# Four experts in two stages: gated products of one expert ahead of the return of the one before, and the rotation's scaling pinned later

## The chip, the cores and the metric

The kernel runs on one core of one Trainium2 chip. Its metric is the time of one execution on the device, in microseconds (us). A core has five engines that run their own queues in order: TensorE (PE, matrix products; PEld is its loading of weights), VectorE (DVE), ScalarE (ACT), GpSimd (POOL) and SyncE (SP, which issues most of the DMAs here). They wait for each other through semaphores. Products are written to PSUM, everything else lies in SBUF or in HBM.

## The reference

Two transformer-like layers on x of 4 x 512 x 512. The first adds a test-time-training attention and a ternary FFN; the second adds a latent attention (MLA) with 16 heads and a rotation of half of each head, and a feed-forward with four experts, where row n goes to expert n mod 4. What the change touches is that last part:

```python
def _L1_ffn_ref(x, gate_up_proj, down_proj):
    B, N, H = x.shape
    E, _, two_I = gate_up_proj.shape
    I = two_I // 2
    x4 = x.reshape(B, N // E, E, H)
    gu = jnp.einsum('bgeh,ehd->bged', x4, gate_up_proj)
    gate, up = (gu[..., :I], gu[..., I:])
    inter = jax.nn.silu(gate) * up
    out = jnp.einsum('bgei,eih->bgeh', inter, down_proj)
    return out.reshape(B, N, H)
...
x = x + _L1_attn_ref(xn, ...) + _L1_ffn_ref(xn, ...)
```

Here E = 4, H = I = 512, all in float32. In the attention, queries and keys are rotated with cos and sin tables before the scores, and the scores are scaled by 1/sqrt(128).

## The kernel before, in words

`trunk_kernel` has three parts: the first layer (to L774), the expert stage (L870 to L983) and the heads of the attention (from L989). The expert stage computes the second layer's feed-forward into four tiles `y[b]`, and beside it prepares what the heads need.

For expert e, `product` (L904) multiplies 128 columns of the weight tile `gu` (512 x 1024, gate and up halves) with the expert's rows `xe`: four matmuls of 512 columns into one PSUM tile, eight rows in the profile. For each of four blocks i there is a gate product `epg` and an up product `epu`; ACT takes the SiLU of the first into `esg` (L950), and VectorE multiplies with the second into `inter` (L951). Then the return: for each batch b, four matmuls of `inter` with the second weight `dn` into `epo` (L957), and VectorE adds that to `y[b]` (L964). So the order on TensorE is products 0, return 0, products 1, return 1, and so on.

Buffers: `epg`, `epu`, `esg`, `inter`, `epo` and `dn` have two each, `gu` of even and of odd experts one each. A product into a buffer waits until the one two places before it has been read: `epu` of block i + 2 waits for `inter` of block i.

The order of most instructions on an engine is chosen by a scheduler when the kernel is built; matmuls of the heads are pinned to the order of the text (`pin`), and so are the large loads of this stage (`fetch`, L880: `xe`, `gu`, `dn`, `y`). All DMAs from SP and ACT take turns on eight completion semaphores: a DMA is issued only when the one eight places ahead of it has landed.

Beside the experts, `if e == 1` (L924) loads what the heads need: `wqr`, `wkr`, biases, the cosine and sine table `trig_k` in four loads (L934), the latents `ckv` and `cq` from `lat_d`, which the first layer's end writes, and starts `first`, a generator (`fold`, L811) that folds the rotations into the heads' weights. `fold` loads straight parts `uk` and `uq` (L816), then five times 16 small loads `raw` (L845), which VectorE transposes into `wt` (L835; one buffer each), and small products `pw` and `pvo` on TensorE; `ow` (L822) are rows of the output weight. After return 1, L969 to L977 put the biases through the rotation and make `trig_q` as `trig_k` times `scale` (L977); it depends on nothing but `trig_k`. It is first read by the heads' `rotate` (L1003).

Of the kernel before, what the change touches and what calls it, by code (L numbers as in the profile page):

```python
# [12 lines left out]
F32 = mybir.dt.float32  # L13
AF = mybir.ActivationFunctionType
# [4 lines left out]
P = 128  # L19
B, L, HS = 4, 512, 512  # L20
# [24 lines left out]
H, D, KVC, QC, RD = 16, 128, 128, 384, 64  # L45
# [6 lines left out]
E, EI = 4, 512  # L52
# [3 lines left out]
def trunk_kernel(ctx: ExitStack, tc: tile.TileContext, a: dict, out: bass.AP):  # L56
    nc = tc.nc
# [20 lines left out]
    def rows_of(ap, b):  # L78
        return ap[b].rearrange("(j e) d -> j e d", e=E)
# [9 lines left out]
    with ExitStack() as px:  # L89
        one = px.enter_context(tc.tile_pool(name="b_one", bufs=1))  # L90
        wk = px.enter_context(tc.tile_pool(name="b_wk", bufs=2))
# [301 lines left out]
        def queries_out(n, wh):  # L393

            po = ps_st.tile([P, NC, 4, K + 1], F32, tag="pso", name=f"pso_{n}")
            for b, r in enumerate(quarters):
                for be in range(NC):
                    mm(po[r, be, :, :K], wh[:, 4 * b + be, :], wq_bd[:, 4 * b + be, :, HD:], be == 0, False)
            return po
# [352 lines left out]
        for n in range(NM):  # L752
            wh = weights_out(n)
            pz = first_product(n, pre)
            po = queries_out(n, wh)
# [25 lines left out]
    y = [ypool.tile([P, E, HS], F32, tag=f"y{b}", name=f"y{b}") for b in range(B)]  # L781
# [5 lines left out]
    scale = 1.0 / math.sqrt(D)  # L787
    trig_k = lat.tile([P, L], F32, tag="trig_k", name="trig_k")
    trig_q = lat.tile([P, L], F32, tag="trig_q", name="trig_q")
# [80 lines left out]
    with ExitStack() as px:  # L870
        one = px.enter_context(tc.tile_pool(name="d_one", bufs=1, reuse_waits="tile"))
        wd = px.enter_context(tc.tile_pool(name="d_wd", bufs=2, reuse_waits="tile"))
        wg = px.enter_context(tc.tile_pool(name="d_wg", bufs=1, reuse_waits="tile"))
        wk = px.enter_context(tc.tile_pool(name="d_wk", bufs=2, reuse_waits="tile"))
        psp = px.enter_context(tc.tile_pool(name="d_ps", bufs=2, space=PSUM))
        ps_gu = px.enter_context(tc.tile_pool(name="d_psgu", bufs=2, space=PSUM))
        gate_w = [one.tile([P, NC, 2 * EI], F32, tag="gu1", name="gu_1")]
        gate_w.insert(0, wg.tile([P, NC, 2 * EI], F32, tag="gu0", name="gu_0"))

        def fetch(**kw):  # L880

            tc.keep_in_program_order(nc.sync.dma_start(**kw))

        def gates(e):
            gu = gate_w[e] if e < 2 else (wg, one)[e % 2].tile([P, NC, 2 * EI], F32, tag=f"gu{e % 2}", name=f"gu_{e}")
            fetch(out=gu, in_=a["gu"][e].rearrange("(c p) o -> p c o", p=P))
            return gu

        def downs(e):
            dn = wd.tile([P, EI // P, HS], F32, tag="dn", name=f"dn_{e}")  # L890
            fetch(out=dn, in_=a["dn"][e].rearrange("(c p) o -> p c o", p=P))
            return dn

        gu = gate_w[0]
        nc.gpsimd.dma_start(out=gu, in_=a["gu"][0].rearrange("(c p) o -> p c o", p=P))
        xe = wg.tile([P, 2 * NCHUNK, NC, E, 32], F32, tag="xe", name="xe")
        for k in range(2 * NCHUNK):
            if k < 2 * NCHUNK - 2:
                nc.gpsimd.dma_start(out=xe[:, k], in_=xe_d[k])
            else:  # L900
                fetch(out=xe[:, k], in_=xe_d[k])
        ws = {0: (gu, downs(0))}

        def product(e, ps, w, col):  # L904
            for c in range(NC):
                nc.tensor.matmul(  # L906
                    ps, lhsT=w[:, c, col : col + P], rhs=xe[:, :, c, e, :], start=(c == 0), stop=(c == NC - 1)
                )

        def by_chunk(ap):  # L910

            return ap.rearrange("p (k b j) -> p k b j", k=NCHUNK, b=B)

        def by_batch(ap):

            return ap.rearrange("p b (k j) -> p k b j", k=NCHUNK)

        for b in range(B):
            fetch(out=y[b], in_=rows_of(yd, b))
        for e in range(E):  # L920
            gu, dn = ws.pop(e)
            if e + 1 < E:
                ws[e + 1] = gates(e + 1), downs(e + 1)
            if e == 1:  # L924
                nc.sync.dma_start(out=wqr, in_=a["W_QR"])
                nc.sync.dma_start(out=wkr, in_=a["W_KR"])
                buv16 = wk.tile([H, D], F32, tag="buv16", name="buv16", bufs=1)
                nc.sync.dma_start(out=buv16, in_=a["b_UV"].rearrange("(h d) -> h d", d=D))
                w0 = group_tiles(lat, 0)
                first = fold(w0, 0, wk, lambda nm: psp.tile([P, 512], F32, tag="pa", name=nm), 1)  # L930
                nc.sync.dma_start(out=buk, in_=a["b_UK"])
                nc.sync.dma_start(out=buq, in_=a["b_UQ"])
                for k in range(E):
                    nc.sync.dma_start(  # L934
                        out=trig_k[RD:, :].rearrange("p (k e j) -> p k e j", k=NCHUNK, e=E)[:, :, k],
                        in_=a["trig"][:, k * P : (k + 1) * P].rearrange("p (k j) -> p k j", k=NCHUNK),
                    )
                nc.sync.dma_start(out=ckv, in_=lat_d[0].rearrange("p b k x -> p b (k x)"))
                for i in range(QC // P):
                    nc.sync.dma_start(out=cq[:, i], in_=lat_d[1 + i].rearrange("p b k x -> p b (k x)"))  # L940
            inter = wk.tile([P, EI // P, B * P], F32, tag="inter", name=f"inter_{e}")
            for i in range(EI // P):
                if e > 1:
                    next(first, None)
                pg = ps_gu.tile([P, B * P], F32, tag="pg", name=f"epg_{e}_{i}")
                product(e, pg, gu, i * P)
                pu = ps_gu.tile([P, B * P], F32, tag="pu", name=f"epu_{e}_{i}")
                product(e, pu, gu, EI + i * P)
                sg = wk.tile([P, B * P], F32, tag="sg", name=f"esg_{e}_{i}")
                nc.scalar.activation(sg, pg, AF.Silu)  # L950
                nc.vector.tensor_mul(  # L951
                    by_batch(inter[:, i].rearrange("p (b j) -> p b j", b=B)), by_chunk(pu), by_chunk(sg)
                )
            for b in range(B):
                po = psp.tile([P, HS], F32, tag="po", name=f"epo_{e}_{b}")
                for i in range(EI // P):
                    nc.tensor.matmul(  # L957
                        po,
                        lhsT=inter[:, i, b * P : (b + 1) * P],
                        rhs=dn[:, i, :],  # L960
                        start=(i == 0),
                        stop=(i == EI // P - 1),
                    )
                nc.vector.tensor_add(y[b][:, e, :], po, y[b][:, e, :])  # L964
            if e in (1, 2):
                next(first, None)
            if e == 1:

                for wr, bias in ((wkr, buk), (wqr, buq)):  # L969
                    pb = psp.tile([P, 512], F32, tag="pa", name="pb")  # L970
                    nc.tensor.matmul(pb[RD:, :H], lhsT=wr, rhs=bias, start=True, stop=True)
                    nc.vector.tensor_copy(bias[RD:, :], pb[RD:, :H])
                pb = psp.tile([P, 512], F32, tag="pa", name="pbuv")
                nc.tensor.transpose(pb[:, :H], buv16, ident[:H, :H])
                nc.vector.tensor_copy(buv, pb[:, :H])
                nc.vector.tensor_scalar_mul(buq[:RD, :], buq[:RD, :], scale)
                nc.vector.tensor_scalar_mul(trig_q[RD:, :], trig_k[RD:, :], scale)  # L977
            if e == 2:
                for b in range(B):
                    pt = psp.tile([P, E, P], F32, tag="pa", name=f"lv_tr_{b}")  # L980
                    for k in range(E):
                        nc.tensor.transpose(pt[:, k, :], ckv[:, b, k * P : (k + 1) * P], ident)
                    nc.scalar.copy(lv[:, b], pt)  # L983

# [2 lines left out]
    with ExitStack() as px:  # L989
        wk = px.enter_context(tc.tile_pool(name="e_wk", bufs=2, reuse_waits="tile"))  # L990
# [145 lines left out]
        ws, cs, qk, probs = {}, {}, {}, {}  # L1136
        folds, outs = iter(()), []
        ws[0] = w0
        for i in range(nu + 1):
            if i < nu:  # L1140
                hg, b, h = units[i]
# [15 lines left out]
            if i >= 3:  # L1157
                hg, b, h = units[i - 3]
# [9 lines left out]
            if 0 <= k < HPG * B:  # L1168
                b, e = divmod(k, HPG)
                nc.gpsimd.tensor_add(y[b][:, e, :], y[b][:, e, :], bo)  # L1170

        b = B - 1
        at = ws[NHG - 1], cs[NHG - 1, b]
        po = {}
# [106 lines left out]
```

## Time and profile before

| | us |
|---|---|
| median of three runs | 2126.29 (2125.87 to 2128.31) |
| the profiled run's own time | 2126.91 |
| its span, first to last instruction | 2125.1 |
| expert stage on TensorE, first `epg` to first `pk` of the heads | 1008.48 to 1193.54 |
| VectorE / ACT / POOL busy, share of the span | 56% / 40% / 24% |
| DMA landing, median: `gu` 2 MB, `dn` 1 MB, `y` 1 MB | 7.8, 5.3, 10.3 |

The page gives one profiled execution. A row of a timeline has the start from the span's beginning, the length, the engine (a q behind it marks its queue, where DMAs are issued), the line, operation, output and inputs, the count, and in brackets the idle time before it with what ended it. A row of the waits has who waited for whom, the sum, how often, and the longest. A wait for several semaphores is put down to the one that came last.

### The profile page before, as it was taken

Reading aid. Unit: us, or ns where it says so; the run is one execution under the profiler, and the core shown is the slowest. Engines: PE = TensorE matmul, PEld = TensorE weight load, DVE = VectorE, ACT = ScalarE, POOL = GpSimd, SP = SyncE. Lnnn points to the kernel's source line nnn. Section 1 sums busy time; section 2 is a strip of 40 time slices with the busy share of each in tenths; the row PEclk is TensorE's granted clock in tenths of the full one; section 3 lists DMA queues with packets and bytes.
Section 4 is the critical chain, followed back from the end, with each engine's and each line's share of the span. In section 5 each row is a group of like instructions: output and inputs, shape, how many; then the busy total and the mean of one; then the engine's idle time right before and its main releaser. Section 6 shows DMA issues by size and latency. Waiting matters only on the chain.

```text
span 2125.1 us, 29355 instructions
## 1 busy us (share of the span) xinstructions
PE 2041.5 (96%) x9932; PEld 1169.6 (55%) x9932; DVE 1199.9 (56%) x2452; ACT 860.5 (40%) x1733; POOL 504.4 (24%) x555
## 2 busy tenths in 40 slices
PE   8999999999999998997899999999999999999999
PEld 6777777767676765744344344444444444444444
DVE  5445656565737475633111485766666665766663
ACT  2334343434334343312001364555545554555552
POOL 5233333323333332302000121111111111142110
PEclk9999999999999999999999999999999999999999
DMA  6546464645454646445831143443334333433332
GB/s 187 161 133 185 120 190 116 193 114 174 138 165 127 183 120 200 116 123 178 300 98 29 29 99 79 93 98 79 78 81 106 78 80 73 101 78 76 91 96 75
DMA packets 336496, 257.19 MB, mean 121 GB/s; under 512 B 107099, under 2 KB 264988, under 8 KB 335324
## 3 DMA queue, kind: packets, MB, share of 16 engines
q1 hardware_dynamic: 322320, 243.89, 42.8%
q10 hardware_dynamic: 11500, 5.32, 0.9%
q0 software_dynamic: 2528, 6.12, 0.8%
q8 instruction: 80, 1.31, 0.3%
q14 instruction: 68, 0.56, 0.1%
HBM read 159.50 MB, written 29.62 MB: 89 GB/s over the span
## 4 chain that ended last, share of the span: by engine, by line
PE 78%; DVE 6%; SPq 6%; DMA 4%; ACT 3%; issue 2%; POOL 1%; ACTq 0%; DVEq 0%; POOLq 0%
PE pj L100 14%; PE pf L100 11%; PE po L1119 9%; PE pc L1106 8%; PE sc L1038 8%; PE pq L1028 7%; PE pd L100 5%; SPq L1098 4%; PE epo L957 3%; PE epu L906 2%; PE pso L100 2%; PE pk L1020 2%; PE epg L906 2%; PE pz L100 2%; SPq L845 1%
## 5 line engine op out<-in xcount | busy, mean ns | idle before, releaser
L1013 POOL TENSOR_TENSOR kT<-t_k,t_k 32x512 f32<-32x512 f32 x64 | 80.7, 1260 | 802.6 <-PE pq L1028 339.9
L1043 ACT ACTIVATE prob<-sc,mx 128x512 f32<-128x512 f32 x256 | 174.3, 683 | 198.9 <-DVE mx L1040 194.1
L1038 PE MATMUL sc<-kT,qT 96*128 96x512 f32 x512 | 230.9, 593 | 1.7 <-ACT prob L1043 1.4
L1119 PE MATMUL po<-vo,ctxT 128*128 128x512 f32 x512 | 230.0, 592 | 0.7 <-ACT ctxT L1108 0.7
L1106 PE MATMUL pc<-prT,lv 128*128 128x512 f32 x496 | 224.8, 596 | 3.2 <-DVE t_q L1003 3.2
L1067 DVE STREAM_TRANSPOSE tt<-prob 128x512 f32<-128x512 f32 x252 | 173.0, 706 | 56.2 <-ACT prob L1048 48.5
L1028 PE MATMUL pq<-cq,uq 128*128 128x512 f32 x384 | 178.0, 600 | 7.3 <-ACT ctxT L1108 7.3
L100 PE MATMUL pf<-xT,wg 128*128 128x256 f32 x704 | 173.5, 389 | 8.2 <-DVE hid L459 7.1
L1048 ACT ACTIVATE prob<-prob,sm 128x512 f32<-128x512 f32 x256 | 176.4, 713 | 0.0
L1040 DVE TENSOR_REDUCE mx<-sc 128x1 f32<-128x512 f32 x256 | 168.2, 678 | 5.8 <-PE sc L1038 3.8
L100 PE MATMUL pf<-xT,wu 128*128 128x256 f32 x704 | 167.5, 381 | 0.0
L1038 PEld LDWEIGHTS sc<-kT,qT 96*128 96x128 f32 x512 | 96.9, 190 | 126.1 <-issue 120.1
L100 PE MATMUL pd<-wd,hid 128*128 128x512 f32 x352 | 164.7, 600 | 1.4 <-DMA wd<-in_wd 1.4
L1119 PEld LDWEIGHTS po<-vo,ctxT 128*128 128x128 f32 x512 | 96.9, 190 | 123.4 <-issue 117.9
L1106 PEld LDWEIGHTS pc<-prT,lv 128*128 128x128 f32 x496 | 94.7, 191 | 123.2 <-issue 118.4
L100 PEld LDWEIGHTS pf<-xT,wg 128*128 128x128 f32 x704 | 132.1, 192 | 34.9 <-DVE hid L459 10.1
L100 PEld LDWEIGHTS pf<-xT,wu 128*128 128x128 f32 x704 | 134.4, 191 | 18.9 <-DMA wu<-in_wu 0.4
L1028 PEld LDWEIGHTS pq<-cq,uq 128*128 128x128 f32 x384 | 73.6, 192 | 101.9 <-issue 90.5
L459 DVE SCALAR_TENSOR_TENSOR hid<-pf,us,sg 128x256 f32<-128x256 f32 x88 | 41.9, 478 | 139.1 <-ACT sg L458 138.4
L297 POOL TENSOR_SCALAR sk<-k,m 128x256 f32<-128x256 f32 x64 | 60.1, 950 | 182.4 <-PE pz L100 173.7
L1003 DVE SCALAR_TENSOR_TENSOR t_k<-pk,b_UK,trig_k 32x512 f32<-32x512 f32 x64 | 47.9, 748 | 90.4 <-ACT kT L1021 89.8
L100 PEld LDWEIGHTS pd<-wd,hid 128*128 128x128 f32 x352 | 63.8, 190 | 61.8 <-issue 48.6
(247 smaller groups left out, 3065.0 us busy)
## 6 DMA issues: line engine op xcount, KB each, us to landing
prT<-tt SPq DMA_DIRECT2D x1008, 64.0 KB, 2.0
wd<-in_wd SPq DMA_DIRECT2D x176, 256.0 KB, 3.0
wg<-in_wg SPq DMA_DIRECT2D x88, 256.0 KB, 2.9
wu<-in_wu SPq DMA_DIRECT2D x88, 256.0 KB, 3.4
rows<-rows SPq DMA_DIRECT2D x128, 66.0 KB, 2.2
kv<-rows SPq DMA_DIRECT2D x32, 264.0 KB, 4.5
gu<-in_gu SPq DMA_DIRECT2D x3, 2048.0 KB, 7.8
xt<-in_x SPq DMA_DIRECT2D x32, 128.0 KB, 3.3
```

Of the source, the lines that this page charges most:

```text
L100: nc.tensor.matmul(out, lhsT=lhsT, rhs=rhs, start=start, stop=stop, skip_group_check=True)
L906: nc.tensor.matmul(ps, lhsT=w[:, c, col : col + P], rhs=xe[:, :, c, e, :], start=(c == 0), stop=(c == NC - 1))
L1013: nc.gpsimd.tensor_sub(t[RD:mid, :], t1[RD:mid, :], t2[RD:mid, :])
L1028: nc.tensor.matmul(pq, lhsT=w[f"uq{i}"][:, h, :], rhs=cq[:, i, b, :], start=(i == 0), stop=(i == nq - 1))
L1038: pin(nc.tensor.matmul(ps, lhsT=qT[:KQ, i * P : (i + 1) * P], rhs=kT[:KQ, :], start=True, stop=True))
L1040: pin(nc.vector.tensor_reduce(mx, ps, AX.X, ALU.max, negate=True))
L1043: pin(nc.scalar.activation(pr, ps, AF.Exp, bias=mx, scale=1.0, accum_out=sm))
L1048: pin(nc.scalar.mul(pr, pr, sm))
L1067: nc.vector.transpose(out=tt[:, :, :, i, :], in_=pr.rearrange("p (kb e j) -> p kb e j", e=2, j=K))
L1098: nc.sync.dma_start(out=prT[32 * kq : 32 * kq + 32, :, qb, :], in_=src[32 * qb : 32 * qb + 32, :, kq, :])
L1106: pin(nc.tensor.matmul(pc, lhsT=lv[:, b, k, :], rhs=prT[:, k, :], start=(k == 0), stop=(k == E - 1)))
L1119: nc.tensor.matmul(po[e], lhsT=ctxT[:, h, e * P : (e + 1) * P], rhs=w["vo"][:, h, :], start=(h == 0), stop=(h == HPG - 1),)
```

## The change

The products of an expert become `hidden(e)`, the return becomes `returned(e)`. The loop calls `hidden(e)` and then `returned(e - 1)`, and `returned(3)` after the loop. So TensorE's order is products 0, products 1, return 0, products 2, return 1, products 3, return 2, return 3. The load of `gu_1` stands ahead of `dn_0`; `gu_{e+2}` is loaded after `hidden(e)`, `dn_{e+1}` at the beginning of `returned(e)`. What was done at the end of `e == 1` (biases, `trig_q`) is done at `e == 2`, after `returned(1)`, and the scaling that makes `trig_q` is kept in the order of the text.

```diff
-        ws = {0: (gu, downs(0))}
+        ws = {0: gu, 1: gates(1)}
+        dns = {0: downs(0)}
...
+        inters = {}
+        def hidden(e):
+            gu = ws.pop(e)
+            inter = inters[e] = wk.tile([P, EI // P, B * P], F32, tag="inter", name=f"inter_{e}")
+            for i in range(EI // P):
+                if e > 1:
+                    next(first, None)
+                pg = ps_gu.tile([P, B * P], F32, tag="pg", name=f"epg_{e}_{i}")
+                product(e, pg, gu, i * P)
+                pu = ps_gu.tile([P, B * P], F32, tag="pu", name=f"epu_{e}_{i}")
+                product(e, pu, gu, EI + i * P)
+                sg = wk.tile([P, B * P], F32, tag="sg", name=f"esg_{e}_{i}")
+                nc.scalar.activation(sg, pg, AF.Silu)
+                nc.vector.tensor_mul(
+                    by_batch(inter[:, i].rearrange("p (b j) -> p b j", b=B)), by_chunk(pu), by_chunk(sg)
+                )
+            if e + 2 < E:
+                ws[e + 2] = gates(e + 2)
+
+        def returned(e):
+            dn, inter = dns.pop(e), inters.pop(e)
+            if e + 1 < E:
+                dns[e + 1] = downs(e + 1)
+            for b in range(B):
+                po = psp.tile([P, HS], F32, tag="po", name=f"epo_{e}_{b}")
...
+                nc.vector.tensor_add(y[b][:, e, :], po, y[b][:, e, :])
+
         for e in range(E):
-            gu, dn = ws.pop(e)
-            if e + 1 < E:
-                ws[e + 1] = gates(e + 1), downs(e + 1)
             if e == 1:
                 nc.sync.dma_start(out=wqr, in_=a["W_QR"])
...
-            inter = wk.tile([P, EI // P, B * P], F32, tag="inter", name=f"inter_{e}")
...
+            hidden(e)
+            if e > 0:
+                returned(e - 1)
             if e in (1, 2):
                 next(first, None)
-            if e == 1:
+            if e == 2:
...
-                nc.vector.tensor_scalar_mul(trig_q[RD:, :], trig_k[RD:, :], scale)
+                tc.keep_in_program_order(nc.vector.tensor_scalar_mul(trig_q[RD:, :], trig_k[RD:, :], scale))
...
+        returned(E - 1)
```

The order that the scheduler makes of it, on VectorE (`inter_e.i` is block i of expert e):

```
before: inter_0.0  trig_q    inter_0.1  inter_0.2  inter_0.3  y y y  wt_0  y  inter_1.0 ...
after:  inter_0.0  inter_0.1 inter_0.2  inter_0.3  inter_1.0  wt_0  inter_1.1  inter_1.2  inter_1.3  y y y y
        inter_2.0  wt_1  inter_2.1  wt_2  inter_2.2  wt_3  inter_2.3  y y y y  wt_4  biases  trig_q ...
```

And of the loads on SP:

```
before: xe  dn_0  y y y y  gu_1  dn_1  W_QR  W_KR  biases  trig_k x4  ckv  cq x3  uk  uq x3
        raw_0 x5  gu_2  raw_0 x11  ow x2  dn_2  raw_1 x16 ...
after:  xe  gu_1  dn_0  y y y y  W_QR  W_KR  biases  trig_k x4  ckv  cq x3  uk  uq x3
        raw_0 x12  gu_2  raw_0 x4  ow x2  raw_1 x16  gu_3  dn_1  raw_2 ...
```

## The prediction

> **What bounds the kernel now.** I read the page first. TensorE is busy for nearly the whole span, so time can only be won where it waits:
>
> ```profile
> span 2125.1 us, 29355 instructions
> PE 2041.5 (96%) x9932; PEld 1169.6 (55%) x9932; DVE 1199.9 (56%) x2452; ACT 860.5 (40%) x1733; POOL 504.4 (24%) x555
> ...
> PEclk9999999999999999999999999999999999999999
> ```
>
> Second, the table of waits over the expert stage (1008 to 1194 us). TensorE has one long wait there, and it is VectorE's product `inter` that it waits for; VectorE itself waited 22.2 us for the rotation's table:
>
> ```profile
> DVE trig_q L977 <- DMA trig_k<-in_trig: 22.2, 1, 22.2
> ...
> PE epu L906 <- DVE inter L951: 7.0, 1, 7.0
> ```
>
> Third, the timelines of VectorE and TensorE around that wait (start, length, line, count, idle before). VectorE runs its queue in order, and the scaling at L977 stands between the first and second gated product of expert 0:
>
> ```profile
> 1015.60 0.69 DVE L951 TENSOR_TENSOR inter<-epu,esg 128x512 f32<-128x512 f32 x1 [5.91 <-issue]
> 1038.50 0.42 DVE L977 TENSOR_SCALAR trig_q<-trig_k 64x512 f32<-64x512 f32 x1 [22.21 <-DMA trig_k<-in_trig]
> 1038.96 1.29 DVE L951 TENSOR_TENSOR inter<-epu,esg 128x512 f32<-128x512 f32 x2
> ```
> ```profile
> 1029.08 3.60 PE L906 MATMUL epg<-xe,gu 128*128 128x512 f32 x8
> 1039.70 5.79 PE L906 MATMUL epu<-xe,gu 128*128 128x512 f32 x8 [7.03 <-DVE inter L951]
> 1045.33 13.90 PE L957 MATMUL epo<-dn,inter 128*128 128x512 f32 x32
> ```
>
> Fourth, the same timelines further on, because the change moves a second load-dependent instruction. The transpose of the first folded weight (L835, `wt_0`) waits for 16 small loads `raw_0`; now it stands where nobody needs VectorE, and it costs nothing:
>
> ```profile
> 1063.67 0.71 DVE L835 STREAM_TRANSPOSE wt<-raw 128x512 f32<-128x512 f32 x1 [7.14 <-DMA raw<-in_W_UK]
> 1064.30 0.65 DVE L964 TENSOR_TENSOR y<-epo,y 128x512 f32<-128x512 f32 x1
> ```
>
> **The change, part by part.** Products (groups of eight rows, one `epg` or `epu`) start 3.43 us apart: 1008.48, 1011.91, ... 1029.08 in TensorE's timeline. A return (`epo`, 32 rows) takes four times that, 13.73.
>
> *Scaling moved behind the second return.* The eighth product was due at 1029.08 + 3.43 = 1032.51. It began at 1039.70, 7.19 late, and took until 1045.33, 5.63 instead of 3.43: the granted clock in the row for 1039.7 to 1046 us is 0.66. Together 7.19 + 2.20 = **9.39 us**. In the changed order `trig_q` follows the biases near 1122 us, when its table has long landed; its 0.42 us lies beside a product of 3.43 (uncovered it would cost 0.42). Moving it removes all 9.39.
>
> *Products of expert 1 before the return of expert 0.* The same 384 rows of matmuls (128 in each of the three groups) run in another order, so TensorE's work doesn't change, nor does ACT's and POOL's; with each product move its `esg` (0.60) and `inter` (0.69), which lie beside the next product. Each `epo` now uses products finished a whole stage before. Two `inter` buffers suffice: `inter_2` is first written after return 0. The removed wait inside a return is worth nothing: `epo` has no idle before it in its group's row.
>
> *Loads.* SP now issues `gu_1` (2 MB) ahead of `dn_0` and the four `y` (1 MB each); `dn_1`, `dn_2`, `dn_3` come later. `gu_1` waited until 1024.36 for the last `lat_d` write to land; now it goes at 1008.67, where `dn_0` went, and is needed at 1008.48 + 27.47 = 1035.95. A 2 MB load took 7.7 to 8.8 us there, so even behind the 5 MB already moving it is in time. `gu_2`, `gu_3` and all later `dn` are issued 20 us or more ahead of use.
>
> *The new wait.* In the changed order `wt_0` stands on VectorE right behind the first `inter` of expert 1 (about 1043) and in front of the second, third and fourth. The second `inter` frees the buffer of the product `epu_1_3`, which TensorE reaches at 1008.48 + 15 x 3.433 = 1059.98. Working back: 0.1 hand-over, 0.69 `inter`, 0.63 from `wt_0` to the next instruction; if `wt_0` starts after **1058.56**, TensorE stands, and behind it everything else. So when does `raw_0` land?
>
> Now, by SP's timeline: the third `trig_k` load waits for `dn_1` (behind `gu_1`, 3 MB issued from 1024.36) and goes at 1035.23, `ckv` at 1036.76, the fifth `raw_0` load at 1050.97, `gu_2` at 1051.51, then the rest; the last four wait for `gu_2` to land and `wt_0` starts at 1063.67. After: a DMA waits for the landing of the one eight places ahead. The place of `dn_1` is taken by `y_3`. Five MB (`dn_0`, four `y`) issued from 1008.67 had landed by 1025.84; two more MB at the 419 GB/s of the window 1016 to 1022 take 5.0 us, so `y_3` lands at 1030.8, 4.4 us ahead of `dn_1` now (1035.2). Everything to the fifth `raw_0` load moves 4.4 earlier. Then seven more raw loads come before `gu_2` instead of after it: `gu_2` at 1051.51 + 7 x 0.48 = 1054.9, minus 4.4 = 1050.5; it took 8.83 to land, and loads queued right behind one landed up to 1.2 later, 0.9 for four: 1060.2, and 0.1 to start. **`wt_0` starts about 1060.3, 1.75 us after the limit**: TensorE loses 1.75 us at `epu_1_3`.
>
> Bounds of this price: 0 if `raw_0` lands 1.8 earlier. Upper end: `y_3` may not be issued until the last `lat_d` write lands (it landed 14.6 us after issue). In 1011 to 1013 that queue moved 13 packets against 346, in 1016 to 1022 it moved 341 against 342; if the first share holds while `gu_1` and `dn_0` move, `y_3` is issued at about 1027 and lands 5.3 later (as a `dn` issued alone), 1032.3: `wt_0` 1.5 later still, a stall of 3.2. I take no bubble: the two-microsecond row is the only one of its kind, and it may be the start-up of the last write. The Trainium skill ("DMA: Bandwidth & Descriptors", Queues, rings and completion order) says that each engine takes turns between queues packet by packet. By that rule, which 341 against 342 bears out and 13 against 346 doesn't, the last write lands early and the price is the 1.75 taken.
>
> After a stall the clock may halve: 2.10 us of idle at 1839.74 was followed by 3.4 us at 0.50, 2.17 at 1565.95 was not, 1.40 and 1.45 were not. 3.4 us at half clock cost 1.7. I take 0 for a stall of 1.75 and 1.7 for the upper end (4.9 together). The Trainium skill ("TensorE: Matmul & The Clock Gate", Part 1: The HAM clock gate) puts the drop at an idle window of some 3.4 us; by it even 3.2 would be free, but the 2.10 row says otherwise.
>
> Other waits: the first `inter` waits for the next-to-last `lat_d` write (landed 1015.32), now with `gu_1` in front; TensorE first needs it at 1025.65, 10 us of slack. `wt_1` to `wt_4` keep the places they have within an expert, with loads issued no later, so they cost nothing as now. In the last two returns, 27.5 us end to end, each `y` addition (0.69) fits in 3.43.
>
> *Sum:* -9.39 + 1.75 = **-7.64 us**. Span 2125.1 becomes 2117.5. The profiled run's own time was 2126.91, 1.8 above its span and 0.6 above the median of 2126.29; from the median, **2118.7**.
>
> **The rivals.**
>
> *Full gain.* `raw_0` lands by 1058.5, because the seven raw loads ahead of `gu_2` delay it less than 0.48 each or `gu_2` needs the 7.7 of `gu_1`. For it: 1.1 of the 1.75 is that one difference. Against: the 8.83 is the same load in the same place. Time 2126.29 - 9.39 = 2116.9.
>
> *The wait only changes its place.* If the loads move no earlier (`y_3` landing at 1035), `wt_0` starts at 1064.7: 6.1 lost at `epu_1_3`, and 2.2 for the clock as now. Gain 1.1, time 2125.2. For it: the queue moves 2 MB more before `y_3`, all four `y` go through it, and VectorE is in order. Against: `dn_1` no longer stands there, and 2 MB cost 5 us, not 9.
>
> *Slower.* One mechanism: the `lat_d` writes are starved behind `gu_1`, each `y` behind a write, and so `ckv` and `raw_0` come later than now. From a `wt_0` at 1058.56 + 7.2 = 1065.8 on, the loss exceeds the gain; at 1070 (`y_3` landing at 1040.5) TensorE loses 11.4 + 2.2 and the time is 2126.29 - 9.39 + 13.6 = 2130.5. Against it: `y_3` would have to land 9.7 us later than worked out with only 7 MB to move since 1008.67.
>
> *The scaling is not really moved* would leave 2126.3; the instruction order as built has it behind the second return, so it gets no chance.
>
> **How the numbers follow.** 0.2% of 2126.29 is 4.25 us, about what a measurement of this kernel can tell from no change: faster means below 2122.0. My forecast (a stall between 0.3 and 5) gets 0.50, full gain 0.28, the wait in a new place (stall over 5) 0.18, slower than now 0.04. Faster: 0.50 + 0.28 and the better third of the third case, 0.84. Within 0.2%: 0.13. Slower by more: 0.03. The range runs from the full gain less 1 us for the half-clock stretches, which can fall otherwise, 2116.0, to the upper end of the price (-9.39 + 4.9, 2121.8) and somewhat into the third case: 2123.
>
> **What would show it.** No wait of VectorE at `trig_q`; the eighth product at 1032.5 right behind the seventh; `gu_1` issued at 1008.7; the start of `epo` of expert 0 near 1063 to 1065. Then the row of `wt_0`: its start, its idle, and a wait of TensorE for `inter` at `epu_1_3` equal to that start minus 1058.56. The third `trig_k` load should go at the landing of `y_3`, near 1030.8. I am wrong if `wt_0` is not what stops TensorE in this stage, if `epu_1_3` waits over 5 us, if a load of `gu` or `dn` becomes the releaser of a product, or if the stage from 1194 us on changes its length by more than 2 us.

## The result and the profile after

| | before | after |
|---|---|---|
| median of five runs, us | 2126.29 (2124.62 to 2128.31) | 2118.65 (2115.88 to 2121.86) |
| the profiled run's own time / its span | 2126.91 / 2125.1 | 2117.2 / 2115.4 |
| first `epg` of the expert stage | 1008.48 | 1007.01 |
| first `pk` of the heads | 1193.54 | 1184.20 |
| stage on TensorE, the one to the other | 185.06 | 177.19 |
| from there to the end of the span | 931.56 | 931.20 |

The ratio is 0.9963, 95% interval 0.9949 to 0.9978: faster by 0.4%. The spans differ by 9.70 us, and the table says where: the stage begins 1.47 earlier (the layer before it, whose instructions are the same), is 7.87 shorter, and 0.36 goes behind it. Only the 7.87 lie in the stage that was changed; the two others are within the spread of all profiles (behind the stage 929.4 to 933.2). The rows that bound the stage, before and after:

```profile
1008.48 3.60 PE L906 MATMUL epg<-xe,gu 128*128 128x512 f32 x8
1193.54 1.10 PE L1020 MATMUL pk<-ckv,uk 128*128 128x512 f32 x2 [0.87 <-DVE y L964]
```
```profile
1007.01 3.60 PE L907 MATMUL epg<-xe,gu 128*128 128x512 f32 x8
1184.20 1.10 PE L1036 MATMUL pk<-ckv,uk 128*128 128x512 f32 x2 [0.88 <-DVE y L957]
```

The page after, first lines (span, then busy time of each engine):

```profile
span 2115.4 us, 29352 instructions
...
PE 2035.5 (96%) x9932; PEld 1167.2 (55%) x9932; DVE 1201.5 (57%) x2452; ACT 861.3 (41%) x1733; POOL 504.9 (24%) x555
```

As before, TensorE is what bounds the kernel. The table of waits of the changed kernel over the expert stage (who, on whom; sum, count, longest):

```profile
DVE wt L835 <- DMA ow<-in_W_O: 16.3, 1, 16.3
...
PE epu L907 <- DVE inter L936: 1.2, 1, 1.2
```

VectorE's 22.2 us at `trig_q` are gone from this table, and TensorE's 7.0 us behind it. In their place VectorE waits 16.3 at `wt_0`, and TensorE 1.2. The timeline of TensorE (start, length, operation, count, idle before), around the eighth product, which was 7.19 late, and at the sixteenth:

```profile
1027.61 3.60 PE L907 MATMUL epg<-xe,gu 128*128 128x512 f32 x8
1031.05 3.60 PE L907 MATMUL epu<-xe,gu 128*128 128x512 f32 x8
1034.48 3.60 PE L907 MATMUL epg<-xe,gu 128*128 128x512 f32 x8
...
1055.08 3.60 PE L907 MATMUL epg<-xe,gu 128*128 128x512 f32 x8
1059.91 3.70 PE L907 MATMUL epu<-xe,gu 128*128 128x512 f32 x8 [1.23 <-DVE inter L936]
1063.45 2.74 PE L950 MATMUL epo<-dn,inter 128*128 128x512 f32 x6
```

The eighth follows the seventh at 3.44. The sixteenth, `epu_1_3`, was due 15 x 3.433 = 51.50 behind the first, at 1058.51, and is 1.40 late; the next begins 3.54 on instead of 3.43. So 1.51 is lost, and the stage is 185.06 - 9.39 + 1.51 = 177.18 (177.19 measured). VectorE's timeline shows who is late, and where the scaling went:

```profile
1041.62 0.69 DVE L936 TENSOR_TENSOR inter<-epu,esg 128x512 f32<-128x512 f32 x1 [6.17 <-PE epu L907]
1058.57 0.71 DVE L835 STREAM_TRANSPOSE wt<-raw 128x512 f32<-128x512 f32 x1 [16.26 <-DMA ow<-in_W_O]
1059.20 1.25 DVE L936 TENSOR_TENSOR inter<-epu,esg 128x512 f32<-128x512 f32 x2
...
1123.98 0.42 DVE L992 TENSOR_SCALAR trig_q<-trig_k 64x512 f32<-64x512 f32 x1
```

`wt_0` stands between the first and the second `inter` of expert 1, waits 16.26 us, and two `inter` go at once behind it. The row names `ow` as releaser, but `wt_0` reads only `raw_0`. The last of those loads landed at 1058.44, 0.13 before it; the second `ow` landed at 1059.05, when `wt_0` was already running. So the name in this bracket is a DMA near in time, not the one awaited. SP's timeline has the issues of `gu_1`, `ckv` and `gu_2`, from which the start of `wt_0` is followed back below:

```profile
1007.21 0.38 SPq L882 DMA_DIRECT2D gu<-in_gu  x1
...
1029.80 0.42 SPq L974 DMA_DIRECT2D ckv<-lat_d  x1
...
1049.06 0.38 SPq L882 DMA_DIRECT2D gu<-in_gu  x1
```

### The profile page after: what moved, and what is told of

The parts are those of the page before. It is cut to its first block, busy times and chain, and to the rows that moved or that the text cites. A ratio compares the mean times of both kernels' runs of the same rounds, so it can differ in the third digit from the quotient of the medians.

```text
span 2115.4 us, 29352 instructions
## 1 busy us (share of the span) xinstructions
PE 2035.5 (96%) x9932; PEld 1167.2 (55%) x9932; DVE 1201.5 (57%) x2452; ACT 861.3 (41%) x1733; POOL 504.9 (24%) x555
## 4 chain that ended last, share of the span: by engine, by line
PE 76%; SPq 7%; DVE 7%; DMA 4%; ACT 3%; issue 2%; POOL 1%; ACTq 0%; DVEq 0%; POOLq 0%
PE pj L100 13%; PE pf L100 12%; PE po L1135 8%; PE sc L1054 8%; PE pc L1122 8%; PE pq L1044 6%; SPq L1114 6%; PE pd L100 5%; PE epg L907 3%; PE epu L907 3%; PE epo L950 3%; PE pso L100 2%; PE pk L1036 2%; PE pz L100 2%; SPq L845 1%
```

## Experiments

Times differ from execution to execution (standard deviation 3.3 to 3.6 us in the kernel before) and between groups of runs, so the stage on TensorE in each profile (first `epg` to first `pk`) decides, and each time is given as a ratio to runs of the kernel before on the same chip. All profiles are in one table first. "Late" is a product's start against its due time from the first `epg` (3.433 a product); "longer" is what the product behind the wait needs over 3.43.

| kernel | stage | late at | late | longer | stage less both |
|---|---|---|---|---|---|
| before | 185.06 | 8th product | 7.19 | 2.20 | 175.67 |
| changed | 177.19 | 16th | 1.40 | 0.11 | 175.68 |
| changed, again (r0) | 176.62 | 16th | 0.83 | 0.10 | 175.69 |
| changed, third (r10) | 176.03 | 16th | 0.24 | 0.11 | 175.68 |
| changed, fourth (r11) | 176.59 | 16th | 0.80 | 0.11 | 175.68 |
| scaling alone (r1 / r9) | 175.68 / 175.67 | none | 0 | 0 | 175.68 / 175.67 |
| stages alone (r2) | 183.43 | 8th | 4.79 | 2.97 | 175.67 |
| stages alone, again (r5) | 181.32 | 8th | 3.84 | 1.80 | 175.68 |
| transpose pinned too (r3 / r8) | 175.69 / 175.68 | none | 0 | 0 | 175.69 / 175.68 |
| transpose one place earlier (r4) | 185.69 | 14th | 7.62 | 2.40 | 175.67 |
| table loaded early (r6) | 175.68 | none | 0 | 0 | 175.68 |
| late loads (r7) | 183.21 | 16th | 5.90 | 1.63 | 175.68 |

The last column is the same for every order of experts and loads: the stage is 175.68 us of work plus one wait and what it costs the product behind it.

### The changed kernel again

No edit.

> The changed kernel itself once more, as the yardstick beside the next three on the same chip. All theories: 2116 to 2122 us, 5 to 10 below the kernel before; the transpose of wt_0 starts within 1 us of the limit plus 1.5, and the sixteenth product (epu_1_3) waits 1 to 2 us for it.

Measured: 2115.38 us median of 8, ratio 0.9957 (0.9942 to 0.9973); `wt_0` 50.98 behind the first `epg`, the sixteenth product 0.83 late (0.66 of it idle) where a wait of 1 to 2 us was expected. The place of the loss is the same and its size smaller.

### The scaling alone

```diff
 # the kernel before
-                nc.vector.tensor_scalar_mul(trig_q[RD:, :], trig_k[RD:, :], scale)
+                tc.keep_in_program_order(nc.vector.tensor_scalar_mul(trig_q[RD:, :], trig_k[RD:, :], scale))
```

> The kernel before with one edit: the scaling that makes trig_q keeps the order of the text, behind return 1. Experts in one stage, loads as before. Theory (the scaling's place in VectorE's queue cost 9.4 us, and nothing else in the change brings time): the eighth product follows the seventh at once, 9.4 us gained, 2116.9 us, so 0 to 2 us faster than the changed kernel. wt_0 waits for its loads until about 1063.7 as before, but it stands behind three y additions and only inter_1.0 is behind it (ready near 1065.7, first needed at 1066.85), so TensorE has no wait over 1 us from 1008 to 1070. Rival (the two stages and the earlier loads are what brings the time; without them the wait only changes its place to wt_0): 2124 us or more, with a wait of TensorE of 5 us or more behind wt_0.

Measured: 2118.16 us (12 runs), ratio 0.9963 (0.9949 to 0.9977), the changed kernel's own ratio. The timeline of TensorE in this kernel, with the eighth product in the second row:

```profile
1031.28 3.60 PE L906 MATMUL epg<-xe,gu 128*128 128x512 f32 x8
1034.71 3.60 PE L906 MATMUL epu<-xe,gu 128*128 128x512 f32 x8
1038.14 13.90 PE L957 MATMUL epo<-dn,inter 128*128 128x512 f32 x32
1051.88 3.60 PE L906 MATMUL epg<-xe,gu 128*128 128x512 f32 x8
```

Nothing stands. The stage is 185.06 - 175.68 = 9.38 shorter, which is the 9.39 worked out for the wait and its half clock. `wt_0` waits here too, and later than in the changed kernel (start 1064.40, 53.73 behind the first `epg`), but no product needs what is behind it in time. So one line brings all of the gain; two stages and the new order of the loads are not needed for it. The rival's 2124 us falls.

### The two stages alone

```diff
 # the changed kernel
-                tc.keep_in_program_order(nc.vector.tensor_scalar_mul(trig_q[RD:, :], trig_k[RD:, :], scale))
+                nc.vector.tensor_scalar_mul(trig_q[RD:, :], trig_k[RD:, :], scale)
```

> The changed kernel without the last edit: the scaling is free again, and the scheduler puts it back between inter_0.0 and inter_0.1. Theory (the scaling costs only as much as its table is late, and the new order of the loads makes the table land near 1031.4 where it was 1038.4): the eighth product is about 1.6 late, which moves the limit of wt_0 1.6 back and takes its stall away; the sum of the two waits is 1.5 to 2 us and the time that of the changed kernel, 2118.7 us, within 2. Rival (it is the pinned place that counts, whatever the loads do): VectorE waits again until the table lands at 1035 or later, 5 us and more lost and the clock halved, 2124 us or more.

Measured: 2118.75 us (12 runs), ratio 0.9969 (0.9952 to 0.9985). The profile is of the longest of these runs, 2127.5. TensorE's row and VectorE's in it:

```profile
1041.26 6.56 PE L907 MATMUL epu<-xe,gu 128*128 128x512 f32 x8 [4.62 <-DVE inter L936]
```
```profile
1040.06 0.42 DVE L992 TENSOR_SCALAR trig_q<-trig_k 64x512 f32<-64x512 f32 x1 [19.80 <-DMA trig_k<-in_trig]
...
1066.76 0.71 DVE L835 STREAM_TRANSPOSE wt<-raw 128x512 f32<-128x512 f32 x1 [11.28 <-DMA ow<-in_W_O]
```

Each expectation is half right. The wait at the table is back, 4.79 late plus 2.97, which is the rival's; `wt_0` no longer costs anything, as the theory said, since the limit moved behind it. The median agrees with the theory and the profile with the rival. The last two `lat_d` writes landed late here, 10.3 and 15.7 us after their issue, and the table 3 us later than forecast. So the next run:

> The two stages without the pinned scaling once more, for a second profile: the twelve times of the first went from 2110 to 2127, and its one profile showed the last two lat_d writes landing 10.3 and 15.7 us after their issue, behind gu_1, where the changed kernel's showed 2.5 and 8.0. Theory (the executions differ in the order of those writes and gu_1, and the scaling pays for it): a profile whose time is below 2116 shows the next-to-last write issued ahead of gu_1, the table landed 24.4 us behind the first epg, and the eighth product 1 to 2 us late; one above 2120 shows the writes late, the table at 27 or later and 4 us or more lost. Rival (the spread comes from other stages): the eighth product is 4 us or more late whatever the time.

Measured: 2118.87 us (10 runs), ratio 0.9971 (0.9953 to 0.9989); the profile is of a run of 2122.2. In it the next-to-last write went ahead of `gu_1` and landed in 3.2 us, and still the eighth product is 3.84 late:

```profile
1033.59 0.42 DVE L992 TENSOR_SCALAR trig_q<-trig_k 64x512 f32<-64x512 f32 x1 [18.85 <-DMA trig_k<-in_trig]
```

That is 26.67 behind the first `epg`; it was 30.02 in the kernel before, and 27.62 in the first profile of this one. So the new order of the loads does bring the table 2.4 to 3.4 us earlier, and that is not enough. That the order of the writes decides was wrong. The 22 times go from 2109.8 to 2127.5 (standard deviation 4.8, against 1.9 of the kernel with the pinned transpose), as if the loss differed from execution to execution; none of the profiles is of a short one. In both profiles the loads, though in the order of the changed kernel, landed later than there: `dn_0` 13.5 and 12.9 us behind the first `epg` instead of 11.1 to 11.6, and `wt_0` began 54.32 and 53.56 behind it. Why is not shown.

### The first transpose pinned too

```diff
 # the changed kernel, in fold
-                pin(
+                (tc.keep_in_program_order if hg == 0 and i == 1 else pin)(
                     nc.vector.transpose(
```

> The changed kernel with the first transpose (wt_0) kept in the order of the text too; the scheduler then has it behind the four y additions of return 0, where only inter_2.0 follows; raw_0 loads as in the changed kernel. Theory (the 1.4 us at epu_1_3 are wt_0 waiting for raw_0 with inter_1.1 behind it): no wait of TensorE at epu_1_3, epo of expert 0 starts 1.5 us earlier counted from the first epg, 2117 us, 1 to 1.5 us below the changed kernel (less than the run to run spread: the rows decide). Rival (epu_1_3 waits for something else, ow or a product): the wait of 1.2 us or more stays at the same place.

Measured: 2113.64 us (6 runs), ratio 0.9946 (0.9930 to 0.9962), the lowest median of all, though the intervals overlap. Sixteenth product and first return in TensorE's timeline, and `wt_0` in VectorE's:

```profile
1055.75 3.60 PE L907 MATMUL epg<-xe,gu 128*128 128x512 f32 x8
1059.18 3.60 PE L907 MATMUL epu<-xe,gu 128*128 128x512 f32 x8
1062.62 0.59 PE L950 MATMUL epo<-dn,inter 128*128 128x512 f32 x1
```
```profile
1077.16 0.70 DVE L835 STREAM_TRANSPOSE wt<-raw 128x512 f32<-128x512 f32 x1
```

The sixteenth product follows the fifteenth at 3.43 and the wait is gone, as is that of VectorE: `wt_0` runs behind the `y` additions, 19 us after its last load landed (1058.39). The stage is 0.35 to 1.51 shorter than in the four profiles of the changed kernel, so this version is ahead of it, and level with the scaling alone (175.69 and 175.68).

### The first transpose one place earlier

The two calls that load `raw_0` and transpose it stand ahead of the products of expert 1, and the first `inter` of expert 1 is kept in the order of the text. Orders of TensorE and of the loads are those of the changed kernel.

```diff
 # the changed kernel with the transpose kept in order
+            if e == 1:
+                next(first, None)
+                next(first, None)
             hidden(e)
...
-                nc.vector.tensor_mul(
+                m = nc.vector.tensor_mul(
...
+                if e == 1 and i == 0:
+                    tc.keep_in_program_order(m)
```

> The changed kernel with wt_0 one place earlier on VectorE: ahead of inter_1.0 instead of behind it; loads and all other orders as in the changed kernel. Theory (TensorE's loss is the lateness of wt_0 against the product whose buffer the next inter frees): inter_1.0 frees the buffer of epu_1_2, two products earlier, so the limit is 6.87 earlier, 43.2 us behind the first epg instead of 50.1; raw_0 lands as before (wt_0 51.0 to 51.6 behind the first epg), epu_1_2 is 7.8 to 8.4 late with the clock halved behind it (2 to 3 more): the stage is 175.7 + 10 to 11.4 = about 186 us, as long as in the kernel before, and the time 8 to 10 us above the changed kernel, 2124 to 2127. Rival (the wait at epu_1_3 is not wt_0's, or VectorE's order has slack here): the stage stays at 176.6 to 177.2 and the time at 2115 to 2119.

Measured: 2126.25 us (10 runs), ratio 1.0008 (0.9990 to 1.0026): the whole gain is lost by one place in VectorE's queue. The profile is of the longest of these runs, 2133.8; its stage is 185.69. TensorE's and VectorE's rows:

```profile
1055.17 3.60 PE L907 MATMUL epg<-xe,gu 128*128 128x512 f32 x8
1066.22 5.98 PE L907 MATMUL epu<-xe,gu 128*128 128x512 f32 x8 [7.46 <-DVE inter L936]
```
```profile
1064.88 0.71 DVE L835 STREAM_TRANSPOSE wt<-raw 128x512 f32<-128x512 f32 x1 [22.48 <-DMA ow<-in_W_O]
```

`wt_0` starts 50.91 behind the first `epg`, as in the changed kernel; less the limit of 43.21 this is 7.70, and 7.62 were lost. The rival, that the wait is not `wt_0`'s, falls.

### Later loads, the same place

```diff
 # the changed kernel, wt_0 kept between inter_1.0 and inter_1.1; this load twice, behind cq and among uq
+                nc.sync.dma_start(
+                    out=lv.rearrange("p b e x -> p b (e x)"), in_=lat_d[0].rearrange("p b k x -> p b (k x)")
+                )
```

> The changed kernel with two more loads of 1 MB from lat_d (into lv, which is overwritten later) behind cq and among the uq loads; gu_2 then goes ahead of all sixteen raw_0, and wt_0 keeps its place between inter_1.0 and inter_1.1. Theory: raw_0 lands 2 to 6 us later, and every microsecond of it is lost at epu_1_3: its lateness is the start of wt_0, counted from the first epg, minus 50.1 (as 1.5 in the changed kernel's first profile and 0.9 in the second), plus 2 to 3 for a halved clock if it is over 3. Rival (the cost is fixed, a hand-over, and not the loads'): 0.7 to 1.5 whatever the start of wt_0.

Measured: 2123.74 us (one run). VectorE's row and TensorE's:

```profile
1065.16 0.71 DVE L835 STREAM_TRANSPOSE wt<-raw 128x512 f32<-128x512 f32 x1 [20.76 <-DMA raw<-in_W_UK]
```
```profile
1066.51 5.23 PE L907 MATMUL epu<-xe,gu 128*128 128x512 f32 x8 [5.73 <-DVE inter L936]
```

`wt_0` starts 56.05 behind the first `epg`; less 50.08 this is 5.97, and 5.90 were lost, plus 1.63 for the clock. Every microsecond of a later load is paid. (This row's bracket names `raw`: here the first `ow` landed 1.3 us behind.)

### The table loaded early

```diff
 # the kernel before; the four loads are taken out of "if e == 1"
+        for k in range(E):
+            fetch(
+                out=trig_k[RD:, :].rearrange("p (k e j) -> p k e j", k=NCHUNK, e=E)[:, :, k],
...
         for b in range(B):
             fetch(out=y[b], in_=rows_of(yd, b))
```

> The kernel before with one edit: the four loads of the rotation's table are issued behind dn_0 and ahead of the four y, so that the table is there early; nothing is pinned, the scheduler puts the scaling ahead of inter_0.0. Theory (not the place but the late table was the cost): the table lands within 10 us of the first epg, the scaling waits less than that and is done before epu_0_2 needs inter_0.0 (17.2 behind the first epg); all 9.39 are gained, the stage is 175.7 to 176 us and the time 2116 to 2118. Rival (small loads among the large ones land as late as those, as the last lat_d write did): the scaling starts 15 us or more behind the first epg, and epu_0_2 waits; the stage is over 180.

Measured: 2117.42 us (10 runs), ratio 0.9960 (0.9946 to 0.9975), stage 175.68. VectorE's rows:

```profile
1017.74 0.42 DVE L977 TENSOR_SCALAR trig_q<-trig_k 64x512 f32<-64x512 f32 x1 [7.66 <-DMA trig_k<-in_trig]
1018.20 0.69 DVE L951 TENSOR_TENSOR inter<-epu,esg 128x512 f32<-128x512 f32 x1
```

The scaling stands even one place earlier than before, ahead of the first `inter`, and waits 7.66 us for its table; nobody needs VectorE that long. The place alone was never the cost: it was the place against the landing. Early data and late work are worth the same here.

### Does anything else differ?

The pinned transpose, the scaling alone and the changed kernel once more, side by side on one chip, with the edits shown above.

> The changed kernel with wt_0 pinned behind return 0, again, beside the next two on one chip. It had 2113.6 us (6 runs), the scaling alone 2118.2 (12 runs), though both profiles show the same 175.7 us in the expert stage. Theory (the difference is spread: the profiles so far begin the stage anywhere from 1004.8 to 1014.0 us and need 929 to 933 us after it): now it is within 2 us of the scaling alone, and its stage is 175.7 us again. Rival (two stages gain 3 us and more elsewhere): again 3 us or more below the scaling alone, with the time after the stage shorter by as much.

> The kernel before with the scaling pinned, again. Theory: stage 175.7 us, time 2115 to 2118, within 2 us of the kernel with the pinned transpose. Rival: 3 us or more above it.

> The changed kernel a third time. Theory: stage 176.5 to 177.3 us with 0.7 to 1.6 lost at epu_1_3, time 0.7 to 2 us above the kernel with the pinned transpose. Rival (the last lat_d write's landing differs from execution to execution and the loss with it): a loss of 2 us or more at epu_1_3 in this profile.

Measured: 2115.41 (6 runs; ratio 0.9954, 0.9939 to 0.9970), 2116.65 (9 runs; 0.9958, 0.9942 to 0.9974) and 2120.18 us (12 runs; 0.9968, 0.9956 to 0.9981). The pinned transpose and the scaling alone are 1.2 apart now, with the same stage: these runs do not show that two stages bring anything elsewhere. The changed kernel came out 4.8 above the pinned transpose, more than expected, though its profile, of a run of 2114.5, shows only 0.35 lost.

> The changed kernel once more, for a profile of one of its longer executions: its 12 last times fall into 2112.7 to 2116.7 (four) and 2119.5 to 2122.6 (eight), while the kernel with the pinned transpose, with the same loads, had none above 2118.8 in 12. Theory (the loads, not the instructions, differ from execution to execution: in the two profiles of the stages alone the first landings were slower and wt_0 began 53.6 and 54.3 us behind the first epg instead of 50.4 to 51.6): in a profile of 2119.5 or more wt_0 begins at 53 or later and epu_1_3 is 3 us or more late with the clock halved behind it, a stage of 180 us or more; in one below 2117.5 the stage is 176 to 177.3. Rival (the longer executions lose their time before or behind the stage): stage 176 to 177.3 in a profile of 2119.5 or more.

Measured: 2114.94 us (8 runs; ratio 0.9961, 0.9946 to 0.9976), all below 2117.1, so no long execution came into the profile:

```profile
1060.99 3.70 PE L907 MATMUL epu<-xe,gu 128*128 128x512 f32 x8 [0.63 <-DVE inter L936]
```

The loss is 0.91, as expected of a short one. Where the long executions of the changed kernel lose their time stays open. The four profiles of it lost 1.51, 0.94, 0.35 and 0.91 at the same product. One candidate is landings as late as in the two profiles of the stages alone: with `wt_0` at 54.32 and 53.56 instead of the limit of 50.08, the sixteenth product would be 4.2 and 3.5 us late, and the half clock would come on top (an estimate; 1.6 to 3.0 in the table). No profile of the changed kernel shows it.

## Why the prediction came out as it did

The forecast was 2118.7 us, -7.64 us of span; measured were 2118.65 and, of the span, -7.87 in the stage. Step by step:

- *The scaling costs 9.39.* Right to 0.01: the scaling alone shortens the stage by 9.38, and so does loading the table early. In its new place it costs nothing (1123.98, no wait).
- *Products ahead of the return cost nothing.* Right: with no wait the stage is 175.68 in both orders.
- *`gu_1` and the later `dn` are in time.* Right: `gu_1` goes 0.20 behind the first `epg`, as `dn_0` did, and no load of `gu` or `dn` releases a product.
- *The limit of `wt_0`.* 1058.56 was 50.08 behind the first `epg`. Right within 0.1 us at two distances from it: lateness worked out as 7.70 and 5.97 was measured as 7.62 and 5.90.
- *The start of `wt_0`.* Forecast 1060.3, or 51.8 behind the first `epg`; 51.56 measured. Two errors cancel in it. `y_3` landed 21.26 behind the first `epg`, not 22.3, so `ckv` went 22.79 behind it where 23.9 was meant; from there to `gu_2` it was 19.3 us instead of 18.1 (the 14.75 of before and seven times 0.48), so `gu_2` went at 42.05, where 42.0 was meant.
- *The price.* 1.75 forecast, 1.51 lost in the first profile. In three more it was 0.35 to 0.94, a mean of 0.93 over the four, so the mechanism was right and the price about twice the mean loss. The forecast took the 8.83 us that `gu_2` had needed before; it needed 8.49 in the first profile and 8.18 in the second. From `gu_2`'s issue to the start of `wt_0` it then took 9.5 and 9.2, where the sum had 9.8. The 0.9 in that sum for the four loads behind `gu_2` is 0.69 in the profile before (1060.34 to 1061.03), and 0.89 in the changed one.
- *The upper end.* The last `lat_d` write was to land late, and `y_3` 1.5 later with it. The write did land 15.0 and 15.7 us after its issue in two profiles with the same loads up to there (r8, r11), and `y_3` was issued 5.8 to 6.1 later than in the first profile, but landed only 0.2 to 0.6 later, 21.5 and 21.8 behind the first `epg`: it took 4.9 us instead of 10.5. In these two the step from late write to late `wt_0` failed. In a third (r2), where the write also took 15.7, `y_3` landed at 24.4, 3.1 later; but there `dn_0` was already 2.3 later, and in r5, where the write took 10.5, `y_3` landed at 23.4. So `wt_0` can come later than the upper end allowed (53.3 behind the first `epg`; 54.32 in r2, 53.56 in r5), and the late write alone is not shown to be the cause.
- *The half clock.* Nothing for a stall of 1.75: right (1.40 and less cost 0.11). 1.7 for 3.2: the nearest shown is 1.80 for 3.84.
- *The first `inter`.* It does not wait for the next-to-last `lat_d` write, as the prediction read it: before, it begins at 1015.60, 0.09 behind the end of its product (1015.51), and in r2 it began at 1019.57, when that write had not landed (1023.26). Nothing in the sum hung on this.

Of the rivals, the full gain is what both kernels with nothing late show, 175.68, so the changed kernel lay 0.35 to 1.51 us from it. "The wait only changes its place" is no feature of this change but one place away from it: 10.02 lost with `wt_0` in front of the first `inter`. For "slower" nothing was seen.

What the forecast did not have is the layer before. The stage began anywhere from 1004.8 to 1014.0 us in fourteen profiles with the same instructions ahead of it, a spread as large as the gain. The 1.47 that it began earlier after the change is part of that, and that the forecast met the median to 0.05 us is luck.

## What to carry to other kernels

On an engine that runs in order, an instruction that waits for a load costs what it is late against the first product that needs anything queued behind it; work out that limit for each place, because one place can be worth the whole gain. Then take the cheapest of the three cures (later work, earlier data, or a place with nothing urgent behind it); here one pinned line did at least all that the restructuring did, and the restructured kernel needs its second waiting instruction pinned as well to get as far. For effects below one per cent compare the stage in the trace, which repeated to 0.02 us here where nothing waited, and use the times only to see that nothing else moved.

## What was not expected of the hardware

A wait of about two microseconds halves the clock in one execution and not in another. Windows of two profiles around a wait of TensorE in the heads (from:to, length, busy time of PE, PEld, DVE, ACT and POOL, granted clock, DMA share and GB/s): the changed kernel (r0), where a wait of 2.08 us that ends at 1554.91 is followed by half clock, and the one with the transpose pinned (r3), where one of 2.24 us that ends at 1327.12 is not.

```profile
1551.31:1554.72 3.41, 1.52 (x8) 0.69 (x7) 2.82 (x7) 3.33 (x8) 0.00 (x0) 1.00 0.40 91
1554.72:1558.14 3.42, 3.23 (x4) 1.52 (x5) 0.99 (x2) 0.99 (x3) 0.00 (x0) 0.50 0.22 34
```
```profile
1322.45:1325.86 3.41, 2.43 (x12) 1.27 (x10) 2.54 (x7) 3.33 (x9) 0.00 (x0) 1.00 0.42 97
1325.86:1329.28 3.42, 2.16 (x5) 1.06 (x6) 1.90 (x3) 2.05 (x5) 0.00 (x0) 1.00 0.27 48
```

At the place of r0's wait, r3 had one of 2.10 with half clock behind it, and r11 one of 2.35 without. The profiles say what differs: where the wait lies. In each of the fourteen, the recorded clock changes only at points that are whole multiples of 3.413 us apart, and the windows above run from one such point to the next. In r0 one window holds 1.89 us of idle time; in r3 a point falls inside the wait and leaves 0.98 on one side and 1.26 on the other. From 1000 us on, all 36 such windows at full clock that had 2.0 us or more without a matmul were followed by half clock, 8 of the 26 with 1.5 to 2.0, and none of the others. This is read from the profiles; no change of the kernel has tested it.

In the expert stage all waits of 3.67 us and more halved the clock, and none of 1.23 and less. What it cost did not follow the wait. It was about half of the half clock that was left when the wait ended: in the kernel before, half clock lasted from 1037.11 to 1043.94 and the wait ended at 1039.70, so 4.24 were left and 2.20 were paid. The others, in the same way (late: left, paid): r2 4.79: 5.79, 2.97; r4 7.62: 4.64, 2.40; r5 3.84: 3.42, 1.80; r7 5.90: 3.11, 1.63.

The Trainium skill ("TensorE: Matmul & The Clock Gate", Part 1: The HAM clock gate) has the drop at an idle window of some 3.4 us; the rows of 3.7 and more agree, the 2.08 doesn't.
